# Four graph layers in one kernel: each engine's order written out by a list scheduler, PSUM split anew, layer 3's norms by a power on GpSimd

## The chip, the cores and the metric

The kernel runs on one core of a Trainium2 chip (trn2). The metric is the device time of one execution in microseconds (us). TensorE (PE in the profile; its weight loads are the row PEld), VectorE (DVE), ScalarE (ACT) and GpSimd (POOL) each work through a queue of their own in order; SyncE (SP) issues most of the DMA transfers. Matmul results land in PSUM, which has 8 banks of 512 float32 columns by 128 partitions.

## The reference

128 graphs of 64 nodes with 512 features (x: 128 x 64 x 512, float32) and a boolean adjacency. Four layers, each `x = x + layer(relu(layernorm(x)), adj)`:

```python
# layers 0 and 2: 4 heads of 64; layer 1: 8 heads, a second layernorm before, self-loops kept
sim  = where(adj, q @ k.T / 8, -max)
out  = softmax(sim) @ v @ Wo + bo
# layer 3: 8 heads of 64
m    = h @ map_w.T + map_b
n    = m / max(norm(m per head), 1e-8)
cos_adj = (n @ n.T, zero where masked) > 0.1
p    = softmax(where(masked, NEG, q @ k.T / 8)) * keep     # q, k from m; keep: node not masked to node 0
a    = cos_adj * p
out  = relu((a @ (h @ gcn_w.T)) @ gcn_W.T / (a.sum(-1) + 1))
```

In layer 3 the boolean `adj` is the score mask, so it masks where it is true.

## The kernel before

Two graphs fill the 128 partitions, and 8 graphs (4 blocks of 128 rows, `TB`) make a step. There are 16 steps per layer and 64 in all. A step has three parts. `stage_a` loads four blocks of x, normalizes them (`scales`, `normalize`) and transposes them on TensorE (`ptr`) into `hT`, features on the partitions. `stage_b` projects: tiles `mm` and `mmv` in PSUM, four matmuls of 128x512 each, copied out by ScalarE and VectorE into q, k and V. In layer 3 it also makes the norms: it squares mT, sums the squares by a matmul with a block of ones (`mmn`), takes the maximum with 1e-16, then Sqrt on ScalarE and a reciprocal on VectorE (L301, L302), and GpSimd multiplies mT by the result (L310). `attention` (or `last` in layer 3) does the scores (`sc`), the masked softmax (predicated copy, max, subtraction, Exp, sum, reciprocal, and a multiplication on GpSimd, L413 or L459), transposes E on TensorE (`ptp`), multiplies by V (`po`), projects with Wo (`mmo`), and adds the residual `xres`, to which GpSimd has added the bias row (L438). Layer 3 also thresholds the cosine scores into Cf and multiplies E by it. The layers pass x through DRAM.

The main loop writes attention of step i, then stage_b of step i + 1, then stage_a of step i + 2. Within that the framework's own scheduler fixes each engine's order by the order of the text and its estimates. A matmul of 512 float32 columns shows as two instructions in the profile.

Each pool has a number of slots; an instruction that writes a new tile waits until the last readers of the slot's old tile are done. PSUM is split 4 + 2 + 2 banks: two tiles `sc` of two banks (scores and `po`), two of one bank for `mm`, `mmv`, `mmo`, two for transposes. Weights go through `wpool` (6 slots), loaded on SP's queue when a layer's first step is done. LayerNorm's `1/sqrt(var + eps)` is a power with exponent -0.5 on GpSimd (L196), of 128 x 2 numbers at a time.

Of the kernel before, what the change touches and what calls it, by code (L numbers as in the profile page):

```python
# [8 lines left out]
F32 = mybir.dt.float32  # L9
# [5 lines left out]
P = 128  # L15
D = 512
# [17 lines left out]

@with_exitstack
def gnn_stack(ctx: ExitStack, tc: tile.TileContext, a: dict, out: bass.AP):
    nc = tc.nc
    x_d = a["x"]
    NG = x_d.shape[0] // (P * TB)

    const = ctx.enter_context(tc.tile_pool(name="const", bufs=1))
    wpool = ctx.enter_context(tc.tile_pool(name="wpool", bufs=6))
    xin = ctx.enter_context(tc.tile_pool(name="xin", bufs=3))
    xres = ctx.enter_context(tc.tile_pool(name="xres", bufs=3))
    hpool = ctx.enter_context(tc.tile_pool(name="hpool", bufs=2))
    qkp = ctx.enter_context(tc.tile_pool(name="qkp", bufs=4))
    mp = ctx.enter_context(tc.tile_pool(name="mp", bufs=2))
    vp = ctx.enter_context(tc.tile_pool(name="vp", bufs=2))
    ep = ctx.enter_context(tc.tile_pool(name="ep", bufs=3))
    cp = ctx.enter_context(tc.tile_pool(name="cp", bufs=2))  # L50
    ptp = ctx.enter_context(tc.tile_pool(name="ptp", bufs=2))
    wk = ctx.enter_context(tc.tile_pool(name="wk", bufs=4))
    nrp = ctx.enter_context(tc.tile_pool(name="nrp", bufs=4))
    mk = ctx.enter_context(tc.tile_pool(name="mk", bufs=2))
    small = ctx.enter_context(tc.tile_pool(name="small", bufs=4))
    dram = ctx.enter_context(tc.tile_pool(name="dram", bufs=1, space=bass.MemoryType.DRAM))
    ps_sc = ctx.enter_context(tc.tile_pool(name="ps_sc", bufs=2, space=bass.MemoryType.PSUM))
    ps_mm = ctx.enter_context(tc.tile_pool(name="ps_mm", bufs=2, space=bass.MemoryType.PSUM))
    ps_tr = ctx.enter_context(tc.tile_pool(name="ps_tr", bufs=2, space=bass.MemoryType.PSUM))

    xs = [[dram.tile([TB * P, D], F32, name=f"x{l}_{s}") for s in range(NG)] for l in range(3)]

# [20 lines left out]
    for g in range(2):  # L83
        r = slice(g * N, (g + 1) * N)
        nc.vector.memset(ones2[r, r], 1.0)
        nc.sync.dma_start(bdw[r, r], a["gcnW3"])
    vecs = const.tile([P, 6, NC], F32, name="vecs")
    nc.sync.dma_start(vecs, a["vecs"].rearrange("p (v c) -> p v c", c=NC))
    gamma, beta, map_b, q_b, k_b, gcn_b = (vecs[:, i, :] for i in range(6))

    W = {}

    def load_w(key, *names):

        t = wpool.tile([P, NC, D], F32, tag="w", name=f"w_{key}")
        at = 0
        for n in names:
            src = a[n]
            o = src.shape[1]
            c = src.shape[0] // P  # L100
            nc.sync.dma_start(t[:, 0:c, at:at + o], src.rearrange("(c p) o -> p c o", p=P))
            at += o
        W[key] = t

    def load_o(key, name, at, t):

        src = a[name]
        v = t[:, 2 * at:2 * at + 2, :]
        nc.sync.dma_start(v, src.rearrange("(c p) o -> p c o", p=P))
        W[key] = v  # L110

    def load_vo(l):
        t = wpool.tile([P, NC, D], F32, tag="w", name=f"w_vo{l}")
        src = a[f"Wv{l}"]
        v = t.rearrange("p c o -> p (c o)")[:, 0:NC * D // 2].rearrange("p (c o) -> p c o", c=NC)
        nc.sync.dma_start(v, src.rearrange("(c p) o -> p c o", p=P))
        W[f"v{l}"] = v
        load_o(f"o{l}", f"Wo{l}", 1, t)

    def load_row(name):  # L120
        src = a[name]
        t = const.tile([P, D], F32, name=name)
        nc.sync.dma_start(t, bass.AP(tensor=src.tensor, offset=src.offset, ap=[[0, P], [1, D]]))
        return t

    bo = {}
    qkb = const.tile([P, 2, NC], F32, name="qkb")

    def load_layer(l):
        if l in (0, 2):  # L130
            load_w(f"qk{l}", f"Wq{l}", f"Wk{l}")
            load_vo(l)
            bo[l] = load_row(f"bo{l}")
        elif l == 1:
            for n in "qkv":
                load_w(f"{n}1", f"W{n}1")
            load_w("o1", "Wo1")
            bo[1] = load_row("bo1")
        else:
            for n in ("map3", "q3", "k3"):  # L140
                load_w(n, n)

    def prepare1():

        bv = small.tile([P, NC], F32, tag="bv", name="bv", bufs=1)
        for i, n in enumerate("qkv"):
            ps = ps_mm.tile([P, NC], F32, tag="mm", name="mmb")
            for oc in range(NC):
                for c in range(NC):
                    nc.tensor.matmul(ps[:, oc:oc + 1], W[f"{n}1"][:, c, oc * P:(oc + 1) * P],  # L150
                                     beta[:, c:c + 1], start=(c == 0), stop=(c == NC - 1))
            nc.vector.tensor_copy(bv if n == "v" else qkb[:, i, :], ps)
            for c in range(NC):
                nc.gpsimd.tensor_scalar_mul(W[f"{n}1"][:, c, :], W[f"{n}1"][:, c, :],
                                            gamma[:, c:c + 1])

        bb = wk.tile([P, NC, P], F32, tag="wk", name="bb")
        nc.vector.tensor_copy(bb, bv[:, :, None].to_broadcast([P, NC, P]))
        ps = ps_mm.tile([P, D], F32, tag="mm", name="mmb")
        for c in range(NC):  # L160
            nc.tensor.matmul(ps, bb[:, c, :], W["o1"][:, c, :], start=(c == 0), stop=(c == NC - 1))
        nc.vector.tensor_add(bo[1], bo[1], ps)

    gcn_row = const.tile([P, D], F32, name="gcn_row")

    def prepare3():

        raw = qkp.tile([P, NC, D], F32, tag="qk", name="gcn3")
        nc.sync.dma_start(raw, a["gcn3"].rearrange("(c p) o -> p c o", p=P))
        t = wpool.tile([P, NC, D], F32, tag="w", name="w_sem3")  # L170
        for f in range(NC):
            ps = ps_mm.tile([P, NC, P], F32, tag="mm", name="mmf")
            for c in range(NC):
                nc.tensor.matmul(ps[:, c, :], raw[:, c, f * P:(f + 1) * P], bdw,
                                 start=True, stop=True)
            nc.scalar.copy(t[:, f, :], ps.rearrange("p c e -> p (c e)"))
        W["sem3"] = t
        bb = wk.tile([P, NC, P], F32, tag="wk", name="bb")
        nc.vector.tensor_copy(bb, gcn_b[:, :, None].to_broadcast([P, NC, P]))
        ps = ps_mm.tile([P, NC, P], F32, tag="mm", name="mmf")  # L180
        for c in range(NC):
            nc.tensor.matmul(ps[:, c, :], bb[:, c, :], bdw, start=True, stop=True)
        nc.vector.tensor_copy(gcn_row, ps.rearrange("p c e -> p (c e)"))


    def scales(views):

        n = len(views)
        mv = small.tile([P, TB, 2], F32, tag="mv", name="mv")
        for t, v in enumerate(views):  # L190
            st = small.tile([P, 6], F32, tag="st", name="st")
            nc.vector.bn_stats(st, v)  # L192
            nc.vector.bn_aggr(mv[:, t, :], st)
        rs = small.tile([P, 2, TB], F32, tag="rs", name="rs")
        nc.vector.tensor_scalar_add(rs[:, 1, :n], mv[:, :n, 1], LN_EPS)  # L195
        nc.gpsimd.tensor_tensor(rs[:, 0, :n], rs[:, 1, :n], mhalf[:, :n], ALU.pow)  # L196
        return mv, rs[:, 0, :]

    def normalize(o, i, mv, rs, t):
        nc.vector.tensor_scalar(o, i, mv[:, t, 0:1], rs[:, t:t + 1], ALU.subtract, ALU.mult)  # L200

    def stage_a(l, s):

        hT = hpool.tile([P, NC, TB * P], F32, tag="h", name="hT")
        for half in range(2):
            ts = (2 * half, 2 * half + 1)
            xt = []
            for t in ts:
                v = xin.tile([P, D], F32, tag="xin", name="xin")
                nc.sync.dma_start(v, x_of(l, s)[t * P:(t + 1) * P, :])  # L210
                xt.append(v)
            mv, rs = scales(xt)
            xn = []
            for i in range(2):
                o = wk.tile([P, D], F32, tag="wk", name="xn")
                normalize(o, xt[i], mv, rs, i)
                if l == 1:
                    nc.vector.tensor_scalar_max(o, o, 0.0)
                xn.append(o)
            if l == 1:  # L220
                mv, rs = scales(xn)
                for i in range(2):
                    normalize(xn[i], xn[i], mv, rs, i)
            for i, t in enumerate(ts):
                pt = ps_tr.tile([P, NC, P], F32, tag="tr", name="ptr")
                for c in range(NC):
                    nc.tensor.transpose(pt[:, c, :], xn[i][:, c * P:(c + 1) * P], ident)  # L227
                o = hT[:, :, t * P:(t + 1) * P]
                nc.scalar.activation(o, pt, AF.Copy if l == 1 else AF.Relu)
        return hT  # L230
# [342 lines left out]
```

## Time and profile before

| | us |
|---|---|
| median of 3 runs (lowest, highest) | 4073.41 (4070.76, 4075.88) |
| profiled execution, own time | 4066.11 |
| its span, first to last instruction | 4064.3 |
| TensorE busy, mean granted clock | 3396.9, 0.916 |
| VectorE, ScalarE, GpSimd busy | 1724.5, 783.3, 660.5 |
| layers by their first and last big matmuls: start and step 0; 0; 1; 2; 3 | 98.7; 692; 1243; 776; 1254 |

A row of the profile's groups reads: source line, engine, operation, output tile <- input tiles, shapes, count | busy us, mean ns of one | idle time of that engine just before, and which instruction ended most of it. The granted clock is the share of full speed that the chip's throttle let TensorE have.

### The profile page before, as it was taken

The numbers are of one execution on the slowest core, as the hardware profiler recorded it, in microseconds if no ns is written. First come the engines' busy times: TensorE is split into PE (matmuls) and PEld (weight loads), VectorE is DVE, ScalarE is ACT, GpSimd is POOL, SyncE is SP. The second block draws the span as 40 slices with busy tenths as digits, with TensorE's granted clock in tenths as the row PEclk, the third lists the DMA queues.
The fourth block names the chain that finished last, engine by engine and source line by source line (L and its number), as shares of the span: only waits on it lengthen the run. The fifth ranks groups of instructions, "written<-read, shape, count | busy, mean of one in ns | idle before, by whom it ended". The sixth has DMA issues, their size and how long they took to land.

```text
span 4064.3 us, 53686 instructions
## 1 busy us (share of the span) xinstructions
PE 3396.9 (84%) x23056; PEld 1826.3 (45%) x23056; DVE 1724.5 (42%) x2657; ACT 783.3 (19%) x1221; POOL 660.5 (16%) x546
## 2 busy tenths in 40 slices
PE   6777777787887888888777777778999989999996
PEld 4454444444443444444444444444444444444443
DVE  3323333434334433432333323333566566566555
ACT  1111111111111111211211111111222222222221
POOL 3111112211111111111111211210111111111111
PEclk8888888898999899899888888889999999999998
DMA  4222222211111111111222222221111111112101
GB/s 139 76 65 70 67 77 80 86 33 38 60 33 38 50 43 38 42 51 33 71 76 80 75 66 70 67 69 47 35 48 50 33 40 54 38 35 59 39 26 35
DMA packets 151246, 226.63 MB, mean 56 GB/s; under 512 B 20064, under 2 KB 64096, under 8 KB 151008
## 3 DMA queue, kind: packets, MB, share of 16 engines
q1 hardware_dynamic: 151008, 223.21, 17.5%
q8 instruction: 180, 2.95, 0.3%
q14 instruction: 58, 0.48, 0.0%
HBM read 156.02 MB, written 67.11 MB: 55 GB/s over the span
## 4 chain that ended last, share of the span: by engine, by line
PE 64%; DVE 20%; DMA 5%; POOL 4%; ACT 3%; SPq 2%; issue 2%; POOLq 0%; DVEq 0%; ACTq 0%
PE mm L237 32%; PE mmv L252 12%; PE mmo L441 10%; DVE sq L302 4%; PE po L428 3%; PE ptp L368 3%; POOL E L413 2%; PE ptr L227 2%; DVE sm L357 2%; DVE E L354 2%; DMA xin<-x 2%; POOL E L459 2%; DVE mx L352 2%; SPq L502 2%; DVE sc L349 2%
## 5 line engine op out<-in xcount | busy, mean ns | idle before, releaser
L368 PE MATMUL ptp<-ident,E 128*128 128x128 f32 x768 | 160.2, 376 | 573.7 <-POOL E L413 511.2
L200 DVE TENSOR_SCALAR xn<-xin,mv,rs 128x512 f32<-128x512 f32 x256 | 147.5, 614 | 830.7 <-PE ptr L227 815.7
L237 PE MATMUL mm<-hT,w_qk 128*128 128x512 f32 x1024 | 450.1, 596 | 4.4 <-DVE xres L443 3.5
L368 PEld LDWEIGHTS ptp<-ident,E 128*128 128x128 f32 x768 | 127.3, 195 | 606.9 <-POOL E L413 517.9
L196 POOL TENSOR_TENSOR rs<-rs,mhalf 128x2 f32<-128x2 f32 x160 | 121.7, 761 | 1458.4 <-DVE rs L195 1014.1
L438 POOL TENSOR_TENSOR xres<-xres,bo 128x512 f32<-128x512 f32 x192 | 243.8, 1270 | 477.3 <-DMA xres<-x 366.4
L237 PEld LDWEIGHTS mm<-hT,w_qk 128*128 128x128 f32 x1024 | 194.5, 191 | 254.0 <-issue 235.2
L443 DVE TENSOR_TENSOR xres<-xres,mmo 128x512 f32<-128x512 f32 x192 | 131.1, 683 | 320.5 <-PE mmo L441 215.6
L413 POOL TENSOR_TENSOR E<-E,sm 128x1024 f32<-128x1024 f32 x64 | 122.8, 1919 | 825.5 <-DVE rs L195 633.4
L237 PE MATMUL mm<-hT,w_map 128*128 128x512 f32 x512 | 247.6, 618 | 0.0
L252 PE MATMUL mmv<-w_sem,hT 128*128 128x512 f32 x512 | 231.3, 599 | 12.2 <-DVE sq L294 9.9
L441 PE MATMUL mmo<-w_o,oT 128*128 128x512 f32 x512 | 233.2, 609 | 3.6 <-ACT oT L434 2.9
L441 PE MATMUL mmo<-w_vo,oT 128*128 128x512 f32 x512 | 229.1, 599 | 8.0 <-ACT oT L434 6.7
L237 PE MATMUL mm<-mT,w_q 128*128 128x512 f32 x512 | 227.5, 598 | 2.8
L252 PE MATMUL mmv<-w_vo,hT 128*128 128x256 f32 x1024 | 226.2, 379 | 0.0
L252 PE MATMUL mmv<-w_v,hT 128*128 128x512 f32 x512 | 222.3, 592 | 0.0
L237 PE MATMUL mm<-mT,w_k 128*128 128x512 f32 x512 | 222.3, 592 | 0.0
L237 PE MATMUL mm<-hT,w_q 128*128 128x512 f32 x512 | 222.3, 592 | 0.0
L237 PE MATMUL mm<-hT,w_k 128*128 128x512 f32 x512 | 222.3, 592 | 0.0
L302 DVE RECIPROCAL sq<-sq 128x512 f32<-128x512 f32 x64 | 213.7, 3339 | 0.0
L252 PEld LDWEIGHTS mmv<-w_vo,hT 128*128 128x128 f32 x1024 | 194.6, 190 | 40.1 <-issue 15.3
L192 DVE BATCH_NORM_STATS2 st<-xin 128x6 f32<-128x512 f32 x256 | 171.0, 678 | 86.4 <-DMA xin<-x 53.5
(106 smaller groups left out, 4030.0 us busy)
## 6 DMA issues: line engine op xcount, KB each, us to landing
x<-xres SPq DMA_DIRECT2D x192, 256.0 KB, 2.1
xin<-x SPq DMA_DIRECT2D x192, 256.0 KB, 2.8
xres<-x SPq DMA_DIRECT2D x128, 256.0 KB, 2.7
xin<-in_x SPq DMA_DIRECT2D x64, 256.0 KB, 2.8
xres<-in_x SPq DMA_DIRECT2D x64, 256.0 KB, 2.7
xr<-x SPq DMA_DIRECT2D x256, 64.0 KB, 2.3
out<-xr SPq DMA_DIRECT2D x256, 64.0 KB, 2.0
adj<-in_adj SPq DMA_DIRECT2D x64, 128.0 KB, 2.2
```

The source lines that it names most:

```text
L192: nc.vector.bn_stats(st, v)
L196: nc.gpsimd.tensor_tensor(rs[:, 0, :n], rs[:, 1, :n], mhalf[:, :n], ALU.pow)
L200: nc.vector.tensor_scalar(o, i, mv[:, t, 0:1], rs[:, t:t + 1], ALU.subtract, ALU.mult)
L237: nc.tensor.matmul(ps, w[:, c, col:col + P], inT[:, c, :], start=(c == 0), stop=(c == NC - 1))
L252: nc.tensor.matmul(ps, hT[:, c, t * P:(t + 1) * P], w[:, c, :], start=(c == 0), stop=(c == NC - 1))
L302: nc.vector.reciprocal(r, r)
L368: nc.tensor.transpose(pt[:, j, :], Ev[:, par * 4 + j, :], ident)
L413: nc.gpsimd.tensor_mul(e, e, sm[:, :, None].to_broadcast([P, 16, N]))
L428: nc.tensor.matmul(po[par * N:(par + 1) * N, g, at:at + N], st["v"][r, t, h * N:(h + 1) * N], pt[r, par, j, a_ * N:(a_ + 1) * N], start=Tr ...
L438: nc.gpsimd.tensor_add(xr, xr, bo[l])
L441: nc.tensor.matmul(ps, oT[:, b * npair + c, :, :].rearrange("p g q -> p (g q)"), wo[:, c, :], start=(c == 0), stop=(c == npair - 1))
L443: nc.vector.tensor_add(xr, xr, ps)
```

## The change

The program is no longer written as a loop over steps. Every part of the work becomes a Python generator, a stream, which yields an engine and a duration in us before each instruction that it emits, or an event that it waits for. `Order.run` takes, over and over, the stream whose next instruction could start first by these durations (ties go to the lower `prio`), and emits it; each slot of a pool is handed on by an event (`Ring`). The whole runs inside `tc.manual_schedule()`, so that each engine issues its instructions in the order in which they were emitted. On the chip nothing is decided anew: an engine that gets to an instruction whose inputs aren't there waits.

```diff
+    def run(self):
+        while self.live:
+            new = [s for s in self.live if s.op is None]
+            if new:
+                self.step(new[0])
+                continue
+            s = min(self.live, key=lambda s: (s.start(self.free), s.prio))
+            eng, dur, lat = s.op
+            at = s.start(self.free)
+            self.free[eng] = at + dur
+            s.ready = at + dur + lat
+            s.last = (eng, at + dur)
+            self.step(s)
...
+def load(us=2.2):
+    return ("sp", 0.35, us)
...
+    r_w = ring("w", 5, [P, NC, D])
+    r_xin = ring("xin", 3, [P, 2, D])
...
+    r_h = ring("h", 2, [P, NC, TB * P])
+    r_qk = ring("qk", 4, [P, NC, TB * P])
+    r_m = ring("m", 2, [P, NC, TB * P])
+    r_v = ring("v", 2, [P, TB, 8 * (N + 1)])
...
+    r_nr = ring("nr", 4, [P, TB * P])
...
+    r_sc = ring("sc", 1, [P, 2, 512], space=ps)
+    r_mm = ring("mm", 4, [P, 512], space=ps)
+    r_tr = ring("tr", 2, [P, NC, P], space=ps)
...
+    def proj_T(o, oc, w, col, inT, left, ev, bias=None, eng="act"):
+
+        p_, e = yield from r_mm.new("mm")
         for c in range(NC):
-            nc.tensor.matmul(ps[:, c, :], raw[:, c, f * P:(f + 1) * P], bdw,
...
+            yield pe(0.857)
+            nc.tensor.matmul(p_, w[:, c, col:col + P], inT[:, c, :],
+                             start=(c == 0), stop=(c == NC - 1))
+        od.spawn(evict(o[:, oc, :], p_, e, bias, eng, left, ev), 0)
...
+    def norms(mT, ready, used):
+        nr = []
         for c in range(NC):
...
+            sq, e = yield from r_nr.new("sq")
+            yield act(0.63)
+            nc.scalar.activation(sq, mT[:, c, :], AF.Square)
+            p_, pe_ = yield from r_mm.new("mmn")
+            yield pe(0.857)
+            nc.tensor.matmul(p_, ones2, sq, start=True, stop=True)
+
+            yield dve(0.69)
+            nc.vector.tensor_scalar_max(sq, p_, 1e-16)
+            pe_.set()
+            yield pool(1.4)
+            nc.gpsimd.tensor_tensor(sq, sq, mhalf[:, 0:1].to_broadcast([P, TB * P]), ALU.pow)
+            nr.append((sq, e))
+        yield used
         for c in range(NC):
...
+            sq, e = nr[c]
+            yield pool(1.3)
+            nc.gpsimd.tensor_mul(mT[:, c, :], mT[:, c, :], sq)
+            e.set()
+        ready.set()
...
+    with tc.manual_schedule():
+        od.spawn(weights(), 4)
+        od.spawn(layernorms(steps), 3)
+        od.spawn(projections(steps), 5)
+        od.spawn(fronts(steps), 1)
+        od.spawn(attentions(steps), 2)
+        od.run()
...
-    adj = np.broadcast_to(adj[None, :, :, None], (2, N, rows // P, 2, 2, N))
+    adj = np.broadcast_to(adj[None], (2, N, rows // P, 2, N))
```

The five streams: `weights` loads and folds the weights through five slots, on ScalarE's DMA queue in place of SP's, layer 1's first ones after the first step's projections. `layernorms` is stage_a, now with one load of 512 KB for two blocks, and from layer 1 on it begins a step when that step's rows of the layer before have been stored. `projections` is stage_b; each eviction from PSUM is a short stream of its own with prio 0. `fronts` does masks, scores, softmax and, in layer 3, the cosine part (`front`); the wait for `n_ready`, set after the last of `norms`' multiplications, stands between the softmax and the cosine scores. `attentions` does the transposes of E and all behind them; residual loads are streams with prio 2.

The norms of layer 3 no longer use Sqrt and the reciprocal: after the maximum, GpSimd takes the power -0.5 of the 128x512 tile, four times a step. The multiplications into mT wait until q's and k's projections have read it (`used`). Masks are kept once per block instead of twice (half the bytes), and the columns of the score tile are ordered by head pair first, so that one mask can be broadcast over them.

## The prediction

> **What bounds the kernel now.** I read the page from the top: busy shares, slices, chain, costliest groups; then the waits of TensorE inside one step of each layer, and the timeline of such a step.
>
> ```profile
> PE 3396.9 (84%) x23056; PEld 1826.3 (45%) x23056; DVE 1724.5 (42%) x2657; ACT 783.3 (19%) x1221; POOL 660.5 (16%) x546
> ...
> PEclk8888888898999899899888888889999999999998
> ...
> PE 64%; DVE 20%; DMA 5%; POOL 4%; ACT 3%; SPq 2%; issue 2%; POOLq 0%; DVEq 0%; ACTq 0%
> ```
>
> TensorE is busy for 84% of the span and carries 64% of the chain that ended last; no other engine is near its limit. Of 667 us in which TensorE idles, most has one name:
>
> ```profile
> L368 PE MATMUL ptp<-ident,E 128*128 128x128 f32 x768 | 160.2, 376 | 573.7 <-POOL E L413 511.2
> ...
> L302 DVE RECIPROCAL sq<-sq 128x512 f32<-128x512 f32 x64 | 213.7, 3339 | 0.0
> ...
> L196 POOL TENSOR_TENSOR rs<-rs,mhalf 128x2 f32<-128x2 f32 x160 | 121.7, 761 | 1458.4 <-DVE rs L195 1014.1
> ```
>
> The transposes of E wait for the softmax to end on GpSimd, 511.2 us. The waits of TensorE in one layer 0 step (329.5 to 375.5; total, times, longest) show it as one long gap:
>
> ```profile
> PE ptp L368 <- POOL E L413: 11.0, 1, 11.0
> ```
>
> The table by stretches (a step of layer 0, of layer 1, of layer 3) gives the work beside it:
>
> ```profile
> core 0: us, PE busy (x) PEld busy (x) DVE busy (x) ACT busy (x) POOL busy (x), PEclk, DMA share, GB/s
> 329.50:375.50 46.00, 34.66 (x233) 21.07 (x232) 14.59 (x26) 7.98 (x14) 8.73 (x7) 0.89 0.21 69
> 955.90:1033.30 77.40, 65.83 (x418) 33.41 (x417) 28.39 (x47) 13.36 (x20) 11.70 (x10) 0.93 0.13 43
> 3063.00:3141.00 78.00, 73.06 (x554) 35.19 (x552) 47.98 (x64) 19.31 (x28) 11.11 (x9) 0.98 0.15 43
> ```
>
> So layers 0 to 2 lose 11 us of each step to one softmax (scores, five VectorE operations, Exp, the GpSimd multiplication) with nothing left for TensorE; layer 3 loses only 4.9 of 78.0.
>
> **The order written out (gain).** Projections become filler (prio 5) for a softmax that runs as a stream of its own (prio 1), with attention behind it as another. All that the filler needs is there: h, q, k and V have two slots per step in flight, and no engine but TensorE is over 50% busy in those layers. If the 11 us fill, a step costs its PE busy time: 34.7 us for layers 0 and 2, 65.8 for layer 1. I add 1 us a step for durations that the scheduler has wrong (it puts 16 of the po matmuls at 0.29 us; 64 took 1.54, so 0.39): 32 x 35.7 = 1142 and 16 x 66.8 = 1069. Before them stay 26 us until the first projection (a start that waits for weights and x) and 22 us of TensorE work to fold gamma and beta. Layers 0 to 2 end at 26 + 22 + 1142 + 1069 = 2259 us; now layer 2 ends at about 2810. The cover for the softmax is the projection of the next step, 20.6 us of PE in layer 0; without it 11 us a step come back, 48 x 11 = 528 us in all.
>
> **Small parts, put at nothing.** One score tile in PSUM instead of two: a tile is held for scores 1.16 + predicate 1.23 + max 1.21 + subtraction 1.21 = 4.8 us, an output tile po for 1.54 + 1.01; in a layer 1 step 2 x 7.4 = 15 of 66 us, in a layer 3 step some 25 of 73, so one slot doesn't bind while projections lie between; if it did, 4.8 us a unit would show. Four mm banks instead of two: a gain of at most the 25 us or so that weight loads wait for evictions. Half-size masks save VectorE 0.3 to 1.2 us a step, beside TensorE work. The 256 x loads of 256 KB become 128 of 512 KB (the 512 KB loads of Wq took 3.4 us against 2.8), fetched a step ahead. The 20 or so weight transfers go from SP's queue to ScalarE's: behind one that waits for its slot stand the PSUM evictions that TensorE needs. SP now waits 31.4 + 13.3 us in front of these loads, so 0 to 45 us is the bound; the order places each after its slot is released, so 0 is taken.
>
> **Layer 3's norms (cost).** Per step this removes 4 reciprocals (4 x 3.34 = 13.4 us of VectorE), 4 Sqrt and two table loads of 1.28 us on ScalarE. VectorE falls from 48.0 to 34.6 us and was not the bound, so this frees little. It adds 4 powers of 128x512 on GpSimd per step, 64 in all. No row has that operation at that size; the scheduler's own entry of 1.4 us is a number in the code, not a measurement. Two rows bound it. Same shape, other operation: the multiplication by the norms, 128x512 in 1.27 us. Same operation, other size: the power of 128x2 in 0.69 us undisturbed, where a GpSimd memset of 128x32 takes 0.155 in all. If all above 0.155 is per column, a column costs (0.692 - 0.155) / 2 = 0.27 us and 512 of them 137 us; if none is, the power costs what a multiplication does. Call it p, from 1.27 to 137 us. The nearer row is that of the same operation (a multiplication shares only the traffic, and a column of power must cost several times its arithmetic), so I weigh it double on a log scale: p = (1.27 x 137 x 137)^(1/3) = 29 us.
>
> What is queued behind a power on GpSimd, which works in order: the next powers, the four multiplications into mT, the E multiplications, and the small power of the LayerNorms two steps ahead. Waiting for those are the cosine scores on TensorE, then Cf and E x Cf on VectorE, then the transposes. GpSimd's step is now 11.1 us of the old work + 4p. I add 5 us for bubbles, as each power needs its matmul and maximum from engines that themselves wait in order: 16.1 + 4p. TensorE's step is 73.1, so up to p = 14.2 us nothing is lost; beyond, GpSimd sets the step. With p = 29 it is 132 us: 16 x 132 = 2112, with 30 us for the lead-in and the last outputs.
>
> The Trainium skill has a rule against this part: "SBUF — State Buffer", section "Who interferes with whom", says that GpSimd and VectorE share a pair of SBUF ports under an exclusive lock for a whole instruction. Its effect is in the trace (columns: start, duration, engine, line):
>
> ```profile
> 3106.15 1.18 DVE L383 TENSOR_TENSOR nf<-nz 128x1024 uint8<-128x1024 uint8 x1
> ...
> 3106.38 2.71 POOL L459 TENSOR_TENSOR E<-E,sm 128x1024 f32<-128x1024 f32 x1 [4.42 <-DVE sm L358]
> ...
> 15.99 2.88 DVE L200 TENSOR_SCALAR xn<-xin,mv,rs 128x512 f32<-128x512 f32 x2 [0.59 <-POOL rs L196]
> ```
>
> The first two overlap and the GpSimd one takes 2.71 us where others take 1.90; in the third, VectorE's two normalizations take 2.88 us beside a GpSimd addition, against 1.00 elsewhere. If a power held VectorE off for its whole length, as the page has it, VectorE would need up to 34.6 + 4p = 151 us a step and the total would be about 300 us more. My sum leaves that out, as the rows show it only for short instructions.
>
> **The sum.** 2259 + 2112 + 30 = 4401 us of span; the profiled execution took 4066.11 for a span of 4064.3, so 4403 for a profiled one, and the median of the runs, 4073.41, lies 7 us above the profiled execution: 4410. A measurement of this kernel can tell some 0.2% (8 us) from no change.
>
> **Rivals.** *The power is cheap enough* (the other sign). One mechanism: a column of power costs less than 46 ns. The sum meets today's 4066 where 2291 + 16 x (16.1 + 4p) = 4066, at p = 23.7 us. Below p = 14.2 TensorE binds layer 3 too: 16 x 73.1 = 1170, and the whole takes 2259 + 1170 + 20 + 9 = about 3460 us. For it: GpSimd is idle 84% of the span and its layer 3 step has 62 us free; half a microsecond for two columns may well be start-up. Against it: a power is many times a multiplication. *The power stays at the per-column price of the 128x2 row.* Then p = 137 and the time 2291 + 16 x 564 = about 11,300 us; at p = 60 it is 6390. For it: nothing shows that start-up is long where a memset takes 0.155. Against it: working one column at a time would waste an engine that multiplies 512 columns in 1.27 us. *The order doesn't fill the gap* (the change doesn't do what it says). Durations off, one score tile, in-order queues: half of the gap stays, 5.5 us for each of 48 steps = 264 us. With a cheap power that gives some 3720 us, with p = 29 about 4670. For it: an engine that reaches a wait early can't take other work. Against it: the missing 11 us stand beside 20 us of projection that depends on nothing in the softmax.
>
> **How the numbers follow.** p between 23.7 and 60 (my case): 0.42, times from 4075 to 6400. p over 60: 0.16. p below 23.7 with the gap filled: 0.33, of which 0.19 below 14.2 at about 3460 and 0.14 between. The gap half filled: 0.07, of which 0.06 with a cheap power. Landing within 8 us: 0.02. Faster: 0.33 + 0.06 = 0.39; same 0.02; slower 0.42 + 0.16 + 0.01 = 0.59. The range leaves out p over 60 and the few times below 3400 (TensorE at full clock in every step): 3400 to 6400. The likeliest case alone spans 4075 to 6400.
>
> **What would show it.** Right: a GpSimd row of 64 powers of 128x512 with a mean near 29 us; GpSimd over 90% busy in layer 3 and 16% or less before; TensorE idle there behind GpSimd, with a lower granted clock; layer 0 steps of 36 us and the wait of the E transposes for GpSimd gone in layers 0 to 2. Wrong in the price: a mean below 14 us and layer 3 steps near 73. Wrong in the order: layer 0 steps still above 41 us, with a wait of TensorE of over 5 us in each. VectorE normalizations or E x Cf stretched to the length of a power would mean that the lock adds to the sum.

## The result, and the profile after

The changed kernel takes 8025.8 us (median of 4 runs) against 4072.1 for the kernel before: a ratio of 1.971 (95% interval 1.967 to 1.974). The profiled span is 8021.7 us. Its page, from the top:

```profile
PE 3269.7 (41%) x23056; PEld 1729.2 (22%) x23056; DVE 1661.7 (21%) x2561; ACT 704.5 (9%) x1125; POOL 5910.7 (74%) x610
...
PE   9999999999903030303123030303032130303030
...
POOL 2221111122398989898898989898998989898988
PEclk9999999999956565656566565656566565656565
...
L538 POOL TENSOR_TENSOR sq<-sq,mhalf 128x512 f32<-128x512 f32 x64 | 5241.9, 81924 | 122.4 <-DVE sq L535 122.4
L385 PE MATMUL ptr<-ident,xn 128*128 128x128 f32 x1024 | 164.0, 286 | 4120.9 <-DVE xn L351 4120.9
```

The slices show two phases: TensorE is full and its clock near full speed for the first eleven (layers 0 to 2), then GpSimd is nearly full, TensorE mostly waits and its clock falls to 0.5 to 0.6. One group says why: 64 powers of 81.9 us each.

In layers 0 to 2 the wait of the E transposes for GpSimd, 511 us before, is down to 12.5 in all (waits of TensorE up to 2170 us: total, times, longest):

```profile
PE ptp L604 <- POOL E L593: 12.5, 26, 1.4
```

The table by stretches shows one step each of layers 0, 1 and 3 (span, then busy PE, PEld, DVE, ACT, POOL, and the clock):

```profile
307.00:340.50 33.50, 33.06 (x234) 19.56 (x233) 16.59 (x28) 8.03 (x15) 9.55 (x8) 1.00 0.28 97
1000.00:1064.00 64.00, 63.01 (x416) 31.07 (x415) 32.11 (x49) 13.50 (x20) 10.34 (x9) 1.00 0.15 51
3644.91:4010.09 365.18, 72.35 (x553) 35.71 (x552) 38.80 (x59) 14.32 (x23) 337.69 (x13) 0.60 0.03 9
```

A layer 0 step fell from 46.0 to 33.5 us and is all TensorE. A layer 3 step rose from 78.0 to 365.2 with nearly the same TensorE work (73.1 us before, 72.4 now). So the low mean clock of 0.60 is that of the waiting: it is 0.51 over the 292 us in which TensorE stands still (3688 to 3980 us) and 1.00 from 3986 to 4012 us, where it is busy all the time. GpSimd's timeline over that step (start, duration) is the whole of it:

```profile
3644.91 327.62 POOL L538 TENSOR_TENSOR sq<-sq,mhalf 128x512 f32<-128x512 f32 x4 [7.08 <-DVE sq L535]
3972.51 4.92 POOL L544 TENSOR_TENSOR mT<-mT,sq 128x512 f32<-128x512 f32 x4
3977.39 0.69 POOL L345 TENSOR_TENSOR rs<-rs,mhalf 128x2 f32<-128x2 f32 x1
3978.05 1.89 POOL L593 TENSOR_TENSOR E<-E,sm 128x1024 f32<-128x1024 f32 x1
3979.89 0.15 POOL L522 MEMSET S<- 128x32 f32 x1
4000.46 1.90 POOL L593 TENSOR_TENSOR E<-E,sm 128x1024 f32<-128x1024 f32 x1 [20.42 <-DVE mv L340]
4002.32 0.70 POOL L345 TENSOR_TENSOR rs<-rs,mhalf 128x2 f32<-128x2 f32 x1
```

Four powers of 327.6 us together, 10.3 us of other work, and two idle times, 20.4 and 7.1 us, 27.5 in all.

### The profile page after: what moved, and what is told of

Its sections match the earlier page's. It is cut to its first block, busy times and chain, and to the rows that moved or that the text cites. A ratio compares the mean times of both kernels' runs of the same rounds, so it can differ in the third digit from the quotient of the medians.

```text
span 8021.7 us, 53389 instructions
## 1 busy us (share of the span) xinstructions
PE 3269.7 (41%) x23056; PEld 1729.2 (22%) x23056; DVE 1661.7 (21%) x2561; ACT 704.5 (9%) x1125; POOL 5910.7 (74%) x610
## 4 chain that ended last, share of the span: by engine, by line
issue 60%; PE 30%; DVE 5%; POOL 2%; DMA 1%; ACT 1%; SPq 0%; POOLq 0%; DVEq 0%; ACTq 0%
PE mm L423 11%; PE mmv L432 8%; PE mmo L712 5%; PE ptr L385 1%; PE sc L564 1%; PE ptp L604 1%; DMA xin<-x 1%; PE po L692 1%; DVE xn L351 1%; DVE mx L580 1%; DVE sc L575 1%; DVE E L583 1%; POOL mT L544 1%; POOL E L593 1%; PE mmn L532 1%
## 5 line engine op out<-in xcount | busy, mean ns | idle before, releaser
L538 POOL TENSOR_TENSOR sq<-sq,mhalf 128x512 f32<-128x512 f32 x64 | 5241.9, 81924 | 122.4 <-DVE sq L535 122.4
L385 PE MATMUL ptr<-ident,xn 128*128 128x128 f32 x1024 | 164.0, 286 | 4120.9 <-DVE xn L351 4120.9
L351 DVE TENSOR_SCALAR xn<-xin,mv,rs 128x512 f32<-128x512 f32 x256 | 219.9, 901 | 4124.2 <-POOL rs L345 4124.2
L385 PEld LDWEIGHTS ptr<-ident,xn 128*128 128x128 f32 x1024 | 128.3, 147 | 4197.9 <-DVE xn L351 4127.6
L649 POOL TENSOR_TENSOR xres<-xres,bo 128x512 f32<-128x512 f32 x192 | 273.5, 1434 | 794.7 <-DMA xres<-x 399.8
L390 ACT ACTIVATE hT<-ptr 128x512 f32<-128x512 f32 x256 | 153.3, 599 | 4815.3 <-PE ptr L385 4815.3
L593 POOL TENSOR_TENSOR E<-E,sm 128x1024 f32<-128x1024 f32 x96 | 186.5, 1943 | 405.9 <-DVE mv L340 285.5
L423 PE MATMUL mm<-hT,w_qk 128*128 128x512 f32 x1024 | 468.1, 600 | 0.7 <-ACT hT L390 0.7
L564 PE MATMUL sc<-mT 64*64 64x64 f32 x2048 | 50.1, 259 | 588.5 <-POOL mT L544 586.8
L423 PE MATMUL mm<-hT,w_k 128*128 128x512 f32 x512 | 242.8, 599 | 0.0
```

Of the source, the lines that this page charges most:

```text
L351: nc.vector.tensor_scalar(o[:, t, :], i[:, t, :], mv[:, t, 0:1], rs[:, t:t + 1], ALU.subtract, ALU.mult)
L385: nc.tensor.transpose(pt[:, c, :], xn[:, t, c * P:(c + 1) * P], ident)
L390: nc.scalar.activation(h[:, :, b * P:(b + 1) * P], pt, AF.Copy if l == 1 else AF.Relu)
L423: nc.tensor.matmul(p_, w[:, c, col:col + P], inT[:, c, :], start=(c == 0), stop=(c == NC - 1))
L538: nc.gpsimd.tensor_tensor(sq, sq, mhalf[:, 0:1].to_broadcast([P, TB * P]), ALU.pow)
L564: nc.tensor.matmul(S[a_ * N:(a_ + 1) * N, par, col], lT[r, c, k], rT[r, c, k], start=True, stop=True)
```

## Experiments

**1. The power alone undone.**

```diff
-            yield pool(1.4)
-            nc.gpsimd.tensor_tensor(sq, sq, mhalf[:, 0:1].to_broadcast([P, TB * P]), ALU.pow)
+            yield act(0.63)
+            nc.scalar.activation(sq, sq, AF.Sqrt)
+            yield dve(3.34)
+            nc.vector.reciprocal(sq, sq)
```

> The change with only the power undone: Sqrt on ScalarE and the reciprocal on VectorE are back, inside the written-out order. Theory (the power's price is the whole loss, the order itself gains): layers 0 to 2 end at 2185 us as in the changed kernel and a layer 3 step falls from 365 us to TensorE's 70 to 74, so 2185 + 16 x 72 + 20, some 3360 us. Rival (the order fixed by wrong durations, or the one score tile, loses time in layer 3 as well): layer 3 steps of 90 us or more, 3650 us or above.

Measured 3306.5 us, 0.812 of the kernel before (0.811 to 0.814). Its page, and the stretch of layer 3:

```profile
PE 3236.4 (98%) x23056; PEld 1713.6 (52%) x23056; DVE 1849.4 (56%) x2625; ACT 779.5 (24%) x1221; POOL 674.1 (20%) x546
...
2185.00:3302.00 1117.00, 1094.84 (x8726) 543.83 (x8724) 788.36 (x957) 293.79 (x433) 163.59 (x139) 0.99 0.16 44
```

A layer 3 step is 1117 / 16 = 69.8 us, layers 0 to 2 end at 2185 as in the changed kernel, and TensorE is 98% busy. So what the change does besides the power gains 766 us, and the power takes that and 3954 us more. The rival (the order fails in layer 3) falls. Experiment 7 takes the PSUM split apart from the order; the smaller masks, the longer loads and the weights' other queue were not undone by themselves, but before the change none of TensorE's longer waits was for a DMA, and the one for the softmax, 511 us, is 11.5 here. It is the fastest kernel of this study.

**2. The power alone done**, in the kernel before: `nc.gpsimd.tensor_tensor(r, r, mhalf[:, 0:1].to_broadcast([P, TB * P]), ALU.pow)` for the Sqrt and reciprocal of L301 and L302.

> The kernel before with only the power put in for Sqrt and reciprocal; the order stays the framework's and PSUM 4 + 2 + 2. Theory (the price alone makes the loss, in any order): GpSimd's layer 3 step is 4 x 81.9 + 11 = 339 us plus a bubble of 5 to 35, so 2810 + 16 x (344 to 374) = 8300 to 8800 us. Rival (a good part of the loss comes from the new order around the power): layer 3 steps well under 339 us can't be, but a total under 8000 would say so.

Measured 9138.4 us (ratio 2.244), a layer 3 step of 399 us: above the range. The price acts in this order too, but the bubble (GpSimd's idle time in a step) is 60 us, not 35 at most. Half of it, some 30 us a step, is a wait of the multiplications into mT for projections that TensorE had not been able to begin: TensorE stood at V's projection, whose result VectorE fetched up to 318 us late. The first row is GpSimd's wait, the second TensorE's:

```profile
POOL mT L309 <- PE mm L237: 433.9, 14, 36.6
...
PE mmv L252 <- DVE S L298: 4428.1, 14, 318.3
```

**3. The price by itself.** Ahead of the kernel before, which then runs unchanged:

```diff
+    for w in (1, 2, 4, 8, 32, 128, 256):
+        pw = pb.tile([P, w], F32, name=f"pw{w}")
+        nc.gpsimd.tensor_tensor(pw, base[:, 0:w], mhalf[:, 0:1].to_broadcast([P, w]), ALU.pow)
+        nc.gpsimd.tensor_tensor(pw, base[:, 0:w], other[:, 0:w], ALU.mult)
...
+    nc.gpsimd.tensor_tensor(long, base, mhalf[:, 0:1].to_broadcast([P, D]), ALU.pow)
...
+    for i in range(50):
+        nc.vector.tensor_scalar(ts, go, 1.5, 0.5, ALU.mult, ALU.add)
+        nc.vector.tensor_tensor(tt, go, other, ALU.mult)
+        nc.vector.tensor_reduce(red, go.rearrange("p (i k) -> p i k", k=N), AX.X, ALU.max)
```

> The kernel before, with a stretch ahead of it that is not part of the computation: on GpSimd powers and multiplications of 1, 2, 4, 8, 32, 128 and 256 columns, then a power of 512 columns while VectorE does 50 rounds of a tensor_scalar (SBUF to SBUF), a product of two SBUF tiles and a reduction. Theory A (a fixed part and a price per column, drawn through 0.69 us at 2 and 81.9 at 512): 0.37 + 0.16 us a column, so 1.6 at 8, 5.5 at 32, 20.8 at 128, 41.1 at 256. Theory B (work in blocks): equal times up to some width, then steps. For VectorE: if GpSimd holds the ports for the whole power, one tensor_scalar or product takes up to 82 us; if only while it reads or writes, all take their 0.4 to 0.7 us but for one at the start.

The groups of GpSimd in that stretch, by form (the last number before the idle time is the mean in ns):

```profile
L523 POOL TENSOR_TENSOR long<-base,mhalf 128x512 f32<-128x512 f32 x1 | 81.9, 81924 | 0.0
L520 POOL TENSOR_TENSOR pw<-base,mhalf 128x256 f32<-128x256 f32 x1 | 41.1, 41123 | 0.0
L520 POOL TENSOR_TENSOR pw<-base,mhalf 128x32 f32<-128x32 f32 x1 | 5.4, 5418 | 0.0
L520 POOL TENSOR_TENSOR pw<-base,mhalf 128x8 f32<-128x8 f32 x1 | 1.6, 1637 | 0.0
L520 POOL TENSOR_TENSOR pw<-base,mhalf 128x2 f32<-128x2 f32 x1 | 0.7, 712 | 0.0
...
L521 POOL TENSOR_TENSOR pw<-base,other 128x256 f32<-128x256 f32 x1 | 0.7, 731 | 0.0
...
L521 POOL TENSOR_TENSOR pw<-base,other 128x2 f32<-128x2 f32 x1 | 0.2, 202 | 0.0
```

A straight line: (81.92 - 0.71) / 510 = 0.159 us a column and 0.39 fixed, with no steps at the widths tried. Theory A holds. By this line the 0.71 us of a power of two columns are 0.39 of start-up and 0.32 for the columns; a multiplication of two columns takes 0.20 in all. The exponent here is one column repeated by broadcasting, the multiplication's second operand is not. At two columns that makes no difference (LayerNorm's power without broadcasting takes 0.69 to 0.70 us); at full width it was not tried. While the power of 82 us ran, VectorE did this:

```profile
75.48 81.92 POOL L523 TENSOR_TENSOR long<-base,mhalf 128x512 f32<-128x512 f32 x1
75.56 1.25 DVE L526 TENSOR_SCALAR ts<-go 128x512 f32<-128x512 f32 x1 [73.30 <-POOL go L522]
76.73 0.68 DVE L527 TENSOR_TENSOR tt<-go,other 128x512 f32<-128x512 f32 x1
77.33 0.67 DVE L528 TENSOR_REDUCE red<-go 128x8 f32<-128x512 f32 x1
77.92 0.41 DVE L526 TENSOR_SCALAR ts<-go 128x512 f32<-128x512 f32 x1
```

Only the first tensor_scalar is longer, by 0.8 us, for a reason that was not tried; the other 49 take 0.41 us and all 50 products 0.68. The Trainium skill ("SBUF — State Buffer", "Who interferes with whom") has the shared port pair held for a whole instruction, with the other engine blocked. No such hold shows during these 82 us, and the measurement decides.

**4. One power a step instead of four**: the other three tiles by Sqrt and reciprocal (`if c == 0` around the two forms of the first experiment).

> The changed kernel with one power per layer 3 step instead of four; the other three tiles take Sqrt and the reciprocal. GpSimd's step is 81.9 + 11 = 93 us plus a bubble, against TensorE's 70. By the bubble of the prediction (5 us): 2185 + 16 x 98 + 30 = 3780 us. By the bubble seen with four powers (27 us): 2185 + 16 x 120 + 20 = 4125 us, no longer faster than the kernel before. If the bubble is smaller because less stands behind a power: between the two.

Measured 4093.6 us, 1.005 (1.003 to 1.007): the 27 us bubble, not 5. GpSimd's timeline has a period of 119.5 us (powers begin at 3019.66 and 3139.13 us): 81.97 + 10.3 of other work + 27.3 idle. A single power of 128x512 a step thus eats all that the order gains.

**5. The scheduler told the true price.** A first kernel, `pool(81.9)` for `pool(1.4)` alone, is no evidence on time: with that price the norms of two steps shared the four norm tiles and waited for each other, and `run` came to its end without them. The program has only 4 of the 64 powers and one of layer 3's 32 softmaxes, and it leaves out all of layer 3's outputs; its 2532.8 us are not those of the whole computation. Its expectation was:

> The changed kernel with one number of the scheduler put right: the power is entered at 81.9 us instead of 1.4. Theory (GpSimd's capacity sets layer 3): its work stays 4 x 81.9 + 11 = 339 us a step, so the time can fall by no more than the 27 us a step in which GpSimd idles, 16 x 27 = 430 us: 7590 to 8030 us. Rival (the wrong estimate made the order bad, and that is the loss): well below 7500 us.

The second takes a step's four norm tiles before its first power:

```diff
+        for c in range(NC):
+            got.append((yield from r_nr.new("sq")))
...
-            yield pool(1.4)
+            yield pool(81.9)
```

> The changed kernel with the power entered at 81.9 us instead of 1.4, and a layer 3 step's four norm tiles taken together before its first power, so that two steps can't hold two each. Theory (GpSimd's capacity sets layer 3): its work stays 339 us a step, so no more than the 27 us of GpSimd's idle time per step can come back: 7590 to 8030 us. Rival (the wrong estimate made the order bad, and that is the loss): well below 7500 us.

Measured 7698.6 us (ratio 1.891), as the theory has it. In layer 3 GpSimd no longer waits before E, and the period is 343.4 us (powers begin at 3557.30 and 3900.70 us), so about 6 us of idle time are left of 27.5. Its only row of waits between 2552 and 7600 us:

```profile
POOL sq L540 <- DVE sq L537: 80.6, 27, 4.0
```

The wrong estimate, together with the order in which the tiles are taken, cost 327 us, 7% of the 4719 us between the changed kernel and the first experiment. The other 93% stay with the right estimate.

**6. Where the bubble comes from.** First, both softmaxes ahead of the wait for the norms (`front`'s loop split in two for layer 3):

> The changed kernel with layer 3's two softmaxes both ahead of the wait for the norms, and the cosine scores of both units after it. Theory (GpSimd's 20.4 us wait in each step is the second unit's softmax, which stands behind the first unit's cosine scores in VectorE's and TensorE's order and in the one score tile): the wait goes, GpSimd idles 7 to 12 us a step instead of 27, so 8026 - 16 x 15 to 20, some 7700 to 7790 us. Rival (the wait has another cause): within 0.5% of 8026.

Measured 8007.8 us: the rival's figure. The waits moved instead of going, from 20.4 + 7.1 to 11.5 + 16.0 us, the period stayed at 365.2:

```profile
3628.82 1.90 POOL L593 TENSOR_TENSOR E<-E,sm 128x1024 f32<-128x1024 f32 x1 [11.47 <-DVE sm L591]
3630.82 0.70 POOL L345 TENSOR_TENSOR rs<-rs,mhalf 128x2 f32<-128x2 f32 x1
3647.50 327.58 POOL L538 TENSOR_TENSOR sq<-sq,mhalf 128x512 f32<-128x512 f32 x4 [15.98 <-DVE f L737]
```

Then, on top of it, layer 3's small LayerNorm power taken off GpSimd:

```diff
+        if l == 3:
+            yield act(0.25)
+            nc.scalar.activation(rs[:, 0, :], rs[:, 1, :], AF.Sqrt)
+            yield dve(0.2)
+            nc.vector.reciprocal(rs[:, 0, :], rs[:, 0, :])
```

> Both softmaxes first, as in the run before, and in layer 3 the LayerNorm's small power goes from GpSimd to Sqrt on ScalarE and a reciprocal on VectorE. Theory (GpSimd's idle 27 us a step is a ring: the small power stands behind the large ones, TensorE's queue waits at the transposes that need it in the midst of the next step's projections, and the next large power needs those projections): the ring opens, GpSimd idles 5 to 10 us a step, 2185 + 16 x (339 + 5 to 10) + 20 = 7710 to 7790 us. Rival (the ring closes elsewhere, at the four norm tiles or the cosine scores): above 7950 us.

Measured 7818.5 us, just above the theory's range, with a period of 351.5: 12 of the 27.5 us go, fewer than expected. So part of the bubble is the ring through the small power. It stands behind the large ones, VectorE waits for it up to 296 us at a time, and TensorE's queue stops at its transposes in the middle of the next step's projections. In the changed kernel (2250 to 8000 us):

```profile
DVE xn L351 <- POOL rs L345: 4106.8, 28, 296.3
PE ptr L385 <- DVE xn L351: 4103.1, 14, 296.3
```

With the small power off GpSimd neither row is among the longer waits. What stays is a wait of 15.3 us of the first large power for VectorE's maximum:

```profile
3945.26 81.92 POOL L544 TENSOR_TENSOR sq<-sq,mhalf 128x512 f32<-128x512 f32 x1 [15.31 <-DVE sq L541]
```

Whether the four norm tiles or the queue order in front of it cause this was not tried.

**7. The PSUM split.** In the order of the first experiment, back to two score tiles and two mm banks; and the new split alone in the kernel before (`ps_sc` 1, `ps_mm` 4).

> The written-out order with Sqrt and reciprocal (the first kernel, 3307 us), but PSUM split as before: two score tiles, two mm banks, two for transposes. Theory (the split is a small part): within 1.5%, 3260 to 3360 us. Rival (four mm banks are what keeps TensorE fed while softmaxes hold VectorE): over 3400 us.

> The kernel before with the split 2 + 4 + 2 alone, the framework's order and its norms. Theory (the order, not the split, fills TensorE's gap): the 11 us gap per step stays, one score tile instead of two may cost a few us where po and the next scores meet: 4030 to 4250 us. Rival (the banks let the projections run under the softmax): below 3950 us.

Measured 3489.0 us (0.856 of before; 5.5% over the first experiment) and 4091.7 us (1.005, 1.003 to 1.007). The split alone brings nothing: TensorE still waits 431 us for the softmax, and 88 more for the one score tile. With the old split the rest of the change still gains 583 us; the split adds 183 to it, all in layer 3, which takes 1299 us with the old split and 1117 with the new; up to 2185 us the two run alike. TensorE's longest waits there are for slots of mm:

```profile
PE mm L423 <- DVE qT L414: 71.3, 14, 5.1
PE mmn L532 <- DVE qT L414: 43.8, 15, 2.9
```

With two banks an eviction that VectorE does late stops TensorE's queue. VectorE is at its busiest in layer 3 (788 of 1117 us in the first experiment).

**8. Another way to the norms**, Ln and Exp on ScalarE.

> As the first kernel, but the norms by Ln and then Exp with scale -0.5, both on ScalarE, so no reciprocal on VectorE. If VectorE is not the bound of layer 3 (34.6 + 13.4 = 48 of 72 us): within 1% of the first kernel. If the reciprocals' 3.3 us stretches delay the softmax chain or the switches of ScalarE's tables cost: faster by 20 to 60 us. If Ln and Exp call for more table loads than Sqrt and Exp: slower by up to 16 x 10 us.

Measured 3366.1 us, 1.8% over the first: the third case. The groups of layer 3 show why (the Sqrt kernel has 16 table loads at its Sqrt and 16 at the softmax's Exp), and so does TensorE's largest wait, for ScalarE's squares, which the Sqrt kernel does not have:

```profile
L540 ACT ACT_TABLE_LOAD x64 | 82.1, 1283 | 1.2
L538 ACT ACT_TABLE_LOAD x63 | 80.8, 1283 | 1.1
...
PE mmn L532 <- ACT sq L529: 50.1, 34, 1.7
```

Each Ln and each Exp of the norms loads a table: 8 x 1.28 us a step. The Trainium skill ("ScalarE: Activation LUTs", "Table sets: the hidden batching unit") names a set that holds both; in this program it was not used. VectorE falls from 788 to 589 us in layer 3 without a gain. That alone would not show that it wasn't the bound, as ScalarE has more to do now; that TensorE is 98% busy in the first experiment does.

## Why the prediction was wrong

*Direction and mechanism were right, the size was not.* Slower was forecast with 0.59, GpSimd as the bound of layer 3, TensorE waiting behind it at a lower clock; all of this is in the profile. The time lies above the range of 3400 to 6400, in the case "p over 60", which had 0.16, between its 6390 us at p = 60 and its 11,300 at p = 137.

*The step that failed is p*, the price of one power of 128x512. It was put between 1.27 and 137 us and drawn down to 29 by weighing in the multiplication's row; it is 81.9. The end of the bracket from the power's own row was 1.7 times too high, the one from the multiplication 64 times too low, so that row should have had no weight: a lower bound from the same operation was needed. The row of 0.69 us could not give one, as it mixes start-up with price, and the trace before has no power of another size. The claim that one column at a time "would waste an engine" was an argument, not a row. With p = 81.9 the prediction's sum is 2259 + 30 + 16 x (16.1 + 327.6) = 7788 us.

*The bubble* was put at 5 us a step and is 27.5: 16 x 22.5 = 360 us. The run with one power has it too (27.3), and the true price brings most of it back. About 12 us of it are the ring through LayerNorm's small power; the cause of the rest stays open.

*Layers 0 to 2* were put at 2259 us and end at 2185, 74 less. The 1 us a step allowed for wrong durations was not needed, and a step's TensorE work itself fell, in layer 0 from 34.7 to 33.1 us. Most of that is in the matmuls right behind the old gap. In the step before, the granted clock fell to 0.50 between 4 and 5 us into the gap and was full again only at 367 us, 4 us after work had begun again; the transposes of E and the matmuls with V there took 2.0 us each, against 1.5 and 1.2 in the changed kernel. By these steps (33.5 and 64.0 us against 35.7 and 66.8) some 115 us go, so about 41 came on outside them; where was not looked into. The rival "the order doesn't fill the gap" is excluded by the layer 0 step of 33.5 us and by TensorE's 98% in the first experiment.

The three together: 7788 + 360 - 74 = 8074 against 8022. Of the other 52 us 30 are those for lead-in and outputs, counted on top of sixteen full steps; the rest is 1 us in each step (366.2 in this sum, 365.2 measured) and a last step that ends some 6 us short.

*Small parts:* the split was put at nothing or a gain of 25 us; with Sqrt and reciprocal for the norms it is worth 183 us, in layer 3. *The lock* was rightly left out of the sum: beside a power of 82 us one VectorE instruction of 150 was 0.8 us longer.

## What to carry to other kernels

A measured duration of a tiny instruction gives no price per element; before an operation is moved to an engine at 256 times the size, run it once at two sizes there. An order fixed at build time got back nearly all of TensorE's idle time where the durations behind it were near (0.81 of the time here). In-order queues spread one long instruction to engines that have nothing to do with it: a LayerNorm power of 0.7 us came behind four of 82, and with it VectorE and TensorE stood still. The wrong entry in the scheduler was the smaller part of the loss (327 of 4719 us). Change one thing at a time where two are sold together: here a gain of 766 us was hidden behind a loss of 4719.

## What the runs showed of the hardware

A GpSimd power cost 0.39 us and 0.159 us for each column of 128 numbers, where a multiplication of 256 columns took 0.73 us in all. During 82 us of it one VectorE instruction of 150 was longer, by 0.8 us. Sqrt and a 3.35 us reciprocal on VectorE, four times a step, left no wait of TensorE for the norms in the first experiment. TensorE's granted clock went with its idle time: 1.00 in full steps, 0.89 with one gap of 11 us in 46, 0.59 to 0.60 where it waits most of the time; within that gap it was 0.50 from its fifth us until 4 us after work had begun again.
